# The last sum of a Mamba block, made by TensorE and copied out by ScalarE instead of added by GpSimd

## The chip, the cores and the metric

The kernel runs on one core of a Trainium2 chip. A core has five engines that each work through their own list of instructions in order and meet at semaphores: TensorE (PE in the profile, with its weight loads shown apart as PEld), VectorE (DVE), ScalarE (ACT), GpSimd (POOL) and SyncE (SP), which issues most of the DMAs. The metric is the device time of one execution in microseconds (us); lower is better. Of a kernel, the median of several executions counts.

## The reference

The reference is a stack of four layers on an input of 2 x 256 x 56 x 56 values: a windowed convolutional attention, a position term, a layer with a six-deep Mamba mixer and a selected-token feed-forward net, and a layer with a causal attention and a mixture of experts. The change touches one addition, the first `t + ...` of layer 2, where `_L2_attn_ref` ends in a root-mean-square norm:

```python
def _L2_attn_ref(x, norm_w, ..., norm_f_w):
    hidden, residual = x, None
    for i in range(n_layer):                      # 6
        residual = hidden if residual is None else hidden + residual
        hidden = rmsnorm(residual, norm_w[i])
        hidden = mamba_mixer(hidden, ...)          # projections, conv, selective scan, gate
    residual = hidden + residual
    return rmsnorm(residual, norm_f_w)
...
t = _to_tokens(x)
t = t + _L2_attn_ref(_ln_t(t), ...)                # <- this sum
t = t + _L2_ffn_ref(_ln_t(t), ...)
```

## The kernel before

The program has three phases: a convolution phase, a Mamba phase (about 700 to 7935 us of the profiled execution), and a tail with the two feed-forward nets and the last attention. All of it is float32.

**The Mamba phase.** A batch's 3136 tokens are cut into 7 chunks of 448 tokens; with 6 layers and 2 batches that makes 84 chunks, numbered by j in the order batch, layer, chunk. Channels lie on the 128 partitions. A chunk has 32 scan steps. A step is: `inputs` (a ScalarE copy of the old state, line 912, and a GpSimd product, line 913), `decays` (two ScalarE exponentials into a PSUM buffer `da`, line 896; three such buffers), `scan` (VectorE, line 934), `product` with C (line 926, on VectorE for 18 steps and on GpSimd for the 14 steps of `on_pool`), `keep` (a ScalarE copy of the last state, line 922), and `gather` (TensorE sums over the states into the PSUM buffer `acc`, line 949; `gate` on VectorE, line 963, takes it out).

**The projections of the next chunk run beside it.** They are pairs of a TensorE product into a PSUM buffer and a ScalarE instruction that takes it out: `u_project`/`u_keep`, `u_convolve`/`u_add`, `z_project`/`z_keep`, `x_project`/`x_keep`, `dt_project`/`dt_keep` (line 737, then two ScalarE instructions, lines 742 and 745), and `dt_add`/`dt_sum`. The last of these adds two tiles by two products with the identity matrix `ident` in one accumulation (lines 754 and 755) and copies the sum out by ScalarE (line 758). All of these pairs use one buffer: `mm()` takes it from the pool `mb_pmm`, which has one buffer, so each product waits until the previous pair's ScalarE instruction is done. Between `dt_keep` and `dt_add` stands `dt_softplus`, an exponential and a logarithm over all four blocks (lines 749 and 750, both ScalarE).

**The order is written out by hand.** Tables (`places`, `steps`, `last`) give each operation a place in units of scan steps within chunk j; all events are sorted by place and issued in that order, so each engine's list follows from the numbers. `dt_keep` of block 0 is at 18.43871, `dt_project` of block 2 at 19.28194, the `decays` of step 20 at 19.736.

**The last norm.** Two chunks after a chunk of the sixth layer, `spare` adds six more operations to chunk j by the table `last`: `l_squares` (5.88), `s_root` (6.46), `s_spread` (9.88), `l_weighted` (10.69), `f_load` (13.48), which loads the block's own input into the tile `t1`, and `l_out` (18.27). `l_weighted` (VectorE, line 803) makes the normed attention output `A["o"]`, 128 x 2 x 448; `l_out` adds it to `t1`, stores the sum to DRAM, and for the first batch starts the load of the next batch's residual into `res`. There are 14 such tails of chunks: 7 in the chunks j = 37 to 43 (first batch), 5 in j = 79 to 83 (second batch), and two in `rest`, a generator that the tail phase runs beside its own start, where `t1` lies in halves of the tile `hz`. The last of the 12, in j = 83, has no projections of a next chunk beside it. `o` shares one buffer with the tile `sq` of the squares.

```python
def l_out(j):
    nc.gpsimd.tensor_tensor(A["t1"], A["t1"], A["o"], ALU.add)          # 845
    nc.sync.dma_start(t2_v[A["b"], :, :, chunk(A["c"], T)], A["t1"])    # 846
    if A["b"] + 1 < B:
        nc.sync.dma_start(res[:, :, chunk(A["c"], T)], r_d[A["b"] + 1][A["c"]])   # 848
```

## Time and profile before

| | |
|---|---|
| median of 3 runs | 8862.84 us (8859.09 to 8866.49) |
| the profiled execution's own time | 8865.82 us |
| its span, first to last instruction | 8863.6 us |
| mean granted TensorE clock | 0.968 |
| DVE busy in the span | 7862.1 us (89%) |
| POOL busy in the span | 7621.6 us (86%) |
| PE busy in the span | 7448.6 us (84%) |
| ACT busy in the span | 6631.1 us (75%) |
| the 14 additions of line 845 | 2.07 to 2.11 us each |

The page of a profile gives busy times over the whole span, and the three phases differ. Between 700 and 7935 us, the Mamba phase, DVE was busy for 7059 of 7235 us, POOL for 7032, ACT for 6164 and PE for 6087. A busy share near one says that an engine is a candidate for the bound; what an engine's idle time waits for says whose lateness it pays for. In lines of the timeline, the columns are the start in us, the duration in us, the engine, the source line, the operation, output and inputs, shapes, and how many instructions are merged; a bracket gives the idle time before the first of them and who ended it. One matmul of the program in float32 appears as two records. A letter q behind an engine's name marks its sequencer (SPq: a DMA issued).

### The profile page before, as it was taken

The numbers are of one execution on the slowest core, as the hardware profiler recorded it, in microseconds if no ns is written. First come the engines' busy times: TensorE is split into PE (matmuls) and PEld (weight loads), VectorE is DVE, ScalarE is ACT, GpSimd is POOL, SyncE is SP. The second block draws the span as 40 slices with busy tenths as digits, with TensorE's granted clock in tenths as the row PEclk, the third lists the DMA queues.
The fourth block names the chain that finished last, engine by engine and source line by source line (L and its number), as shares of the span: only waits on it lengthen the run. The fifth ranks groups of instructions, "written<-read, shape, count | busy, mean of one in ns | idle before, by whom it ended". The sixth has DMA issues, their size and how long they took to land.

```text
span 8863.6 us, 106477 instructions
## 1 busy us (share of the span) xinstructions
PE 7448.6 (84%) x32350; PEld 3271.9 (37%) x32350; DVE 7862.1 (89%) x7216; ACT 6631.1 (75%) x15748; POOL 7621.6 (86%) x5327
## 2 busy tenths in 40 slices
PE   9988888888888888888888888888888888867986
PEld 6553333333333333333333333333333333325774
DVE  3339999999999999999999999999999999985763
ACT  1128888888888888888888888888888888863432
POOL 2329999999999999999999999999999999972336
PEclk9999999999999999999999999999999999978988
DMA  2235565565655565656566556556556565543224
GB/s 85 84 115 128 132 137 129 132 137 130 137 131 129 136 133 129 135 135 146 136 136 136 132 128 138 132 130 135 132 132 134 127 138 130 133 119 93 71 81 131
DMA packets 700485, 1118.30 MB, mean 126 GB/s; under 512 B 80508, under 2 KB 678083, under 8 KB 699907
## 3 DMA queue, kind: packets, MB, share of 16 engines
q1 hardware_dynamic: 685128, 1074.33, 52.4%
q0 software_dynamic: 14784, 37.18, 1.6%
q8 instruction: 257, 4.21, 0.2%
q14 instruction: 316, 2.59, 0.1%
HBM read 892.62 MB, written 218.60 MB: 125 GB/s over the span
## 4 chain that ended last, share of the span: by engine, by line
PE 44%; ACT 34%; DVE 12%; issue 7%; POOL 1%; DMA 1%; SPq 0%; ACTq 0%; POOLq 0%; DVEq 0%
ACT da L896 12%; PE mm L683 9%; PE mm L665 8%; PE mm L821 6%; DVE da L934 4%; PE acc L949 4%; DVE x L934 4%; ACT dt L742 2%; DVE x L926 2%; ACT hz L695 2%; ACT dt L750 2%; PE mm L754 2%; ACT hz L700 2%; ACT dt L749 2%; ACT dt L758 1%
## 5 line engine op out<-in xcount | busy, mean ns | idle before, releaser
L913 POOL TENSOR_TENSOR x<-dtur,bc 128x900 f32<-128x900 f32 x2688 | 4711.2, 1786 | 6.9 <-DMA dtu_d<-dtu 6.6
L896 ACT ACTIVATE da<-dtr,am 128x451 f32<-128x451 f32 x5376 | 3417.3, 641 | 322.4 <-DVE x L934 151.3
L934 DVE TENSOR_TENSOR_SCAN da<-da,x 128x902 f32<-128x902 f32 x1512 | 3040.3, 2031 | 97.4 <-ACT da L896 74.9
L934 DVE TENSOR_TENSOR_SCAN x<-da,x 128x902 f32<-128x902 f32 x1176 | 2343.5, 2020 | 45.8 <-ACT da L896 37.5
L926 POOL TENSOR_TENSOR x<-x,bc 128x896 f32<-128x896 f32 x1176 | 2074.3, 1777 | 80.7 <-DVE x L934 80.7
L926 DVE TENSOR_TENSOR x<-da,bc 128x896 f32<-128x896 f32 x1512 | 1606.2, 1076 | 19.1 <-ACT state L922 7.7
L949 PE MATMUL acc<-x,sum_w 128*32 128x448 f32 x10752 | 1380.2, 567 | 47.6 <-DVE x L926 30.2
L683 PE MATMUL mm<-u,w_cv 128*128 128x448 f32 x2656 | 1091.9, 553 | 67.1 <-ACT tail L678 56.9
L665 PE MATMUL mm<-xn,w_z 128*128 128x448 f32 x1332 | 588.8, 564 | 197.5 <-ACT dt L758 117.3
L683 PEld LDWEIGHTS mm<-u,w_cv 128*128 128x128 f32 x2656 | 478.4, 190 | 677.8 <-issue 373.8
L665 PE MATMUL mm<-xn,w_u 128*128 128x448 f32 x1328 | 580.8, 560 | 123.3 <-ACT hz L695 114.7
L821 PE MATMUL mm<-hz,w_out 128*128 128x448 f32 x1344 | 553.0, 554 | 107.9 <-ACT tail L678 56.3
L949 PEld LDWEIGHTS acc<-x,sum_w 128*32 128x32 f32 x10752 | 265.4, 111 | 954.9 <-issue 730.2
L754 PE MATMUL mm<-dt,mb_ident 128*128 128x448 f32 x666 | 342.6, 596 | 262.9 <-ACT state L922 148.6
L737 PE MATMUL mm<-xd,w_dt 128*128 128x448 f32 x664 | 341.1, 596 | 216.8 <-ACT dtu L745 128.5
L766 POOL TENSOR_TENSOR dtu<-dt,hz 128x448 f32<-128x448 f32 x336 | 329.4, 980 | 129.7 <-PE mm L755 81.9
L912 ACT COPY x<-state 128x2 f32<-128x2 f32 x2688 | 437.0, 187 | 0.0
L665 PEld LDWEIGHTS mm<-xn,w_z 128*128 128x128 f32 x1332 | 226.1, 189 | 566.4 <-ACT dt L758 237.8
L665 PEld LDWEIGHTS mm<-xn,w_u 128*128 128x128 f32 x1328 | 232.1, 189 | 460.4 <-ACT hz L695 226.7
L821 PEld LDWEIGHTS mm<-hz,w_out 128*128 128x128 f32 x1344 | 243.0, 191 | 417.5 <-issue 189.1
L695 ACT ACTIVATE hz<-mm,vec 128x448 f32<-128x448 f32 x332 | 209.0, 629 | 238.5 <-PE mm L683 234.0
L944 PE MATMUL acc<-hz,w_sk 128*128 128x448 f32 x672 | 347.4, 601 | 30.5 <-DVE hz L963 30.5
(366 smaller groups left out, 9520.3 us busy)
## 6 DMA issues: line engine op xcount, KB each, us to landing
dtr<-dt_d SPq DMA_DIRECT2D x1344, 224.0 KB, 4.4
dtur<-dtu_d SPq DMA_DIRECT2D x1344, 224.0 KB, 6.7
bc<-bc_d SPq DMA_DIRECT2D x336, 448.0 KB, 7.9
dt_d<-dt SPq DMA_DIRECT2D x336, 224.0 KB, 6.2
dtu_d<-dtu SPq DMA_DIRECT2D x336, 224.0 KB, 2.0
z_d<-out SPq DMA_DIRECT2D x56, 256.0 KB, 2.1
xg<-in_x SPq DMA_DIRECT2D x26, 448.0 KB, 9.2
bm<-in_edge SPq DMA_DIRECT2D x16, 539.0 KB, 4.4
```

The lines of the kernel that those rows point to most:

```text
L665: nc.tensor.matmul(ps, lhsT=w[:, k, chunk(d, P)], rhs=Q["xn"][:, k, :], start=(k == 0), stop=(k == 1),)
L683: nc.tensor.matmul(ps, lhsT=w_cv[:, 4 * d + k, :], rhs=M["u", d][:, k : k + T], start=(k == 0), stop=(k == 3),)
L695: nc.scalar.activation(hz(j)[:, d, :], M["mm"], AF.Identity, bias=layer_of(j + 1)["cb"][:, d : d + 1])
L754: nc.tensor.matmul(ps, lhsT=ident, rhs=M["dt"][:, d, :], start=True, stop=False)
L821: nc.tensor.matmul(ps, lhsT=layer_of(j - 1)["w_out"][:, d, chunk(k, P)], rhs=gated(j - 1)[:, d, :], start=(d == 0), stop=False,)
L896: nc.scalar.activation(D[i][:, chunk(g, R)], dtr[:, 2 * pr + g, :], AF.Exp, scale=L["am"][:, col : col + 1],)
L912: nc.scalar.copy(x[:, :, 0:1], states(i))
L913: nc.gpsimd.tensor_tensor(x[:, :, 1:], Q[k][1][:, 2 * pr : 2 * pr + 2, :], wide(Q["bc"][:, ng, :]), ALU.mult)
L926: engine.tensor_tensor(both(X[i])[:, :, 1 : T + 1], both(h)[:, :, 1 : T + 1], wide(QS[j]["bc"][:, 4 + ng, :T]), ALU.mult,)
L934: nc.vector.tensor_tensor_scan(h, D[i], X[i], 0.0, ALU.mult, ALU.add)
L944: nc.tensor.matmul(acc[0][:, :T], lhsT=L["w_sk"][:, k, :], rhs=Q["hz"][:, k, :], start=True, stop=False,)
L949: nc.tensor.matmul(acc[0][chunk(g, HD), :T], lhsT=sum_w, rhs=both(X[i - 1 + g // 2])[:, g % 2, 1 : T + 1], start=False, stop=(ng == 3), ti ...
```

## The change

The addition of `l_out` is made, for each half k of the tile, by two TensorE products with the identity into the buffer of `mm()`, and a ScalarE copy takes the sum back into `t1`. The place of `l_out` in the table `last` moves from 18.26579 to 18.60000, which is behind `dt_keep` of block 0 instead of between its `dt_project` and it. The two DMAs are as before; they now wait for the copy.

```diff
     def l_out(j):
-        nc.gpsimd.tensor_tensor(A["t1"], A["t1"], A["o"], ALU.add)
+        for k in range(2):
+            ps = M["mm"] = mm()[:, :T]
+            nc.tensor.matmul(ps, lhsT=ident, rhs=A["t1"][:, k, :], start=True, stop=False)
+            nc.tensor.matmul(ps, lhsT=ident, rhs=A["o"][:, k, :], start=False, stop=True)
+            nc.scalar.copy(A["t1"][:, k, :], ps)
         nc.sync.dma_start(t2_v[A["b"], :, :, chunk(A["c"], T)], A["t1"])
...
-        f_load: 13.47985, l_out: 18.26579,
+        f_load: 13.47985, l_out: 18.60000,
```

In the instruction lists, the changed kernel's ScalarE has the two copies, one straight behind the other, after line 745 of block 0 and one state copy of line 912, and ahead of a state copy of line 922 and the `decays` of step 20. TensorE has the four products between a `gather` and `dt_project` of block 2.

## The prediction

> **What bounds the kernel now.** I read the page's busy times first, then the waits of VectorE in the stretch of the Mamba phase that holds both groups of affected chunks (3810 to 7800 us), then the view of line 845 itself, and last the timeline of one affected place, engine by engine.

> ```profile
> PE 7448.6 (84%) x32350; PEld 3271.9 (37%) x32350; DVE 7862.1 (89%) x7216; ACT 6631.1 (75%) x15748; POOL 7621.6 (86%) x5327
> ...
> DVE da L934 <- ACT da L896: 38.9, 95, 0.8
> DVE x L934 <- ACT da L896: 22.7, 57, 1.8
> DVE o L803 <- PE mm L795: 17.4, 11, 1.6
> ...
> DVE da L934 <- POOL x L913: 2.0, 7, 0.3
> ```

> VectorE and GpSimd look equally full, but they are not equally the bound. In 3990 us VectorE waited 61.6 us for ScalarE's exponentials (line 896) and 2.0 us for GpSimd. So VectorE sets the pace, and what makes it late is ScalarE and the TensorE products that ScalarE waits for.

> ```profile
> L845 POOL TENSOR_TENSOR t<-t,o x12: 2086/2093/2109, 3901.2 to 7893.5; 128x896 f32<-128x896 f32 x12
> ...
> who waited for it (us, times):
>   ACT sq L776: 3.4, 1
> ```

> Of the twelve additions inside chunks, one made another engine wait. GpSimd has room behind the others: after the one at 3901.24 it idles 0.35 us for TensorE at 3917.59 and 2.60 us for VectorE at 3978.34. The chunk distance agrees. The starts of the SiLU of line 700 lie 85.31 us apart in ordinary chunks and 89.22 in affected ones. Of those 3.9 us, VectorE's timeline has 1.59 as the wait of line 803 for line 795 and 1.27 as line 803's own work at 3969.59, and most of the rest as two waits for ScalarE (0.42 at 3978.68, 0.34 at 3898.81); none is a wait for line 845.

> Now ScalarE where the copies go (j = 37):

> ```profile
> 3903.97 0.62 ACT L745 ACTIVATE u<-mm,above 128x448 f32<-128x448 f32 x1
> 3904.48 0.19 ACT L912 COPY x<-state 128x2 f32<-128x2 f32 x1
> 3904.56 0.17 ACT L922 COPY state<-da 128x2 f32<-128x2 f32 x1
> 3904.76 1.31 ACT L896 ACTIVATE da<-dtr,am 128x451 f32<-128x451 f32 x2
> ...
> 3909.61 1.79 ACT L749 ACTIVATE dt<-dt,cap 128x1792 f32<-128x1792 f32 x1
> 3911.43 1.79 ACT L750 ACTIVATE dt<-dt,one_col 128x1792 f32<-128x1792 f32 x1
> 3913.13 0.14 ACT L922 COPY state<-da 128x2 f32<-128x2 f32 x1
> 3913.31 1.32 ACT L896 ACTIVATE da<-dtr,am 128x451 f32<-128x451 f32 x2
> ...
> 3915.09 0.53 ACT L758 COPY dt<-mm 128x448 f32<-128x448 f32 x1 [0.20 <-PE mm L755]
> ```

> No bracket stands between 3904 and 3915: ScalarE has no idle time in these 11 us. And VectorE at the end of that run is already waiting for it:

> ```profile
> 3912.33 2.09 DVE L926 TENSOR_TENSOR x<-da,bc 128x896 f32<-128x896 f32 x2
> 3914.72 2.04 DVE L934 TENSOR_TENSOR_SCAN da<-da,x 128x902 f32<-128x902 f32 x1 [0.31 <-ACT da L896]
> ```

> **The change, part by part.** *Removed:* 14 additions on GpSimd, 12 x 2.09 + 2 x 2.07 = 29 us of its time. On the path I count them at nothing, because VectorE waited 2.0 us in all for GpSimd over both groups. Bounds: a gain of 12 x 2.09 = 25.1 us if GpSimd paced the chunks, nothing if VectorE does; I take nothing, by the waits.

> [...]

> *Added:* four matmuls and two copies per call. The nearest row is the same form of pair, `dt_add`/`dt_sum`:

> ```profile
> 3913.28 1.02 PE L754 MATMUL mm<-dt,mb_ident 128*128 128x448 f32 x2 [0.51 <-ACT state L922]
> 3914.14 0.91 PE L755 MATMUL mm<-u,mb_ident 128*128 128x448 f32 x2
> 3915.67 1.02 PE L754 MATMUL mm<-dt,mb_ident 128*128 128x448 f32 x2 [0.62 <-ACT state L922]
> ```

> From one pair to the next is 2.39 us: 1.81 from the first product's start to the copy (3913.28 to 3915.09), then 0.58 from the copy's start to the next product (to 3915.67), because `mm` has a single buffer. The busy time added is small (two copies of 0.53 on ScalarE), but both copies stand next to each other in ScalarE's list, so ScalarE stands still through both products. Step by step: `dt_project` of block 2 started at 3904.64 when line 745 gave the buffer back; the new product starts there instead. Copy one at 3904.64 + 1.81 = 3906.45, second product at 3907.03, copy two at 3908.84, and the next ScalarE instruction 0.43 us later (as 3915.09 to 3915.52) at 3909.27. It ran at 3904.56 before, so all that is queued behind is 4.71 us late. TensorE's `dt_project` of block 2 is late by 2 x 2.39 = 4.78, just inside ScalarE's own lateness.

> *Who waits behind it:* three pairs of `decays`, the `dt_keep` of two blocks, the softplus. VectorE has work in hand at first: the scan at 3908.33 uses the pair of 3904.76; a pair is ready 1.41 us after its start (3913.31 to 3914.72), so that scan starts at 3904.76 + 4.71 + 1.41 = 3910.88, 2.55 late. The next (pair at 3907.33) starts at 3913.45 instead of 3910.30, 3.15 late. The one at 3914.72 already waited, so it takes the whole 4.71. After it the brackets of ScalarE wait for TensorE's pairs, which are late by the same amount, and VectorE is again the full engine, with less than 3 us of waits in the rest of the chunk; I see nothing that gives time back. Bounds of one call: 0 (all regained) to 4.78; I take 4.71.

> *Moved:* the place 18.27 to 18.60 puts the call behind `dt_keep`, so `mm` stays in order. SP's two DMAs (3903.35 and 3903.83) now wait until about 3909.4; the next DMA in SP's list is `dt_d` at 3915.65, itself 4.7 us later then, so nothing queues up. The reloaded `res` is read three chunks later. `o` comes free when TensorE has read it, which only j = 83 notices.

> *The sum.* Eleven calls (j = 37 to 43 and 79 to 82) have the pattern above: 11 x 4.71 = 51.8 us. In j = 83 ScalarE waited 3.41 us for line 845 and VectorE 2.53 us for ScalarE; the copies take the place of that wait. Two pairs at full clock (4.8 us from about 7889.9) or half clock (some 8) put it between 1.2 us earlier and 2 later; I take 0. In `rest` the first call sits ahead of the tail's transposes on TensorE. They were paced by landings until 7945.25, so 4.8 to 8 us of products from 7935 are mostly covered: 0 to 4, I take 1.5. The second stands ahead of 14 ScalarE rows (line 1423, about 0.51 us each, 7961.41 to 7973.0) that used to run during the wait for `o` at 7966.3. ScalarE gets to them at about 7970.4 to 7973; 28 rows then end at 7984.7 to 7987.3 instead of 7981.7, and the chain of waits runs through the loads issued just behind (7982.13): 3 to 5.5, less if VectorE is what counts, so 0 to 5.5; I take 3.5. Total 51.8 + 0 + 1.5 + 3.5 = 56.8 us. On the profiled 8865.82 that gives 8922.6; on the median of 8862.84, 3 us lower, **8919.6 us** (+0.64%).

> Of the tail's clock: the granted clock was 0.50 from 7937 to 7949. [...]

> **Rivals.**
> - *GpSimd is the bound after all* (faster). Place: line 845 between products of line 913. For it: 98% busy in these stretches (586 of 600 us). Against it: 2.0 us of waits. It decides if the stall's 4.71 us is covered and VectorE follows GpSimd: 8862.8 - 25.1 = 8838, with the tail's 5 8843.
> - *The stall is hidden.* VectorE's work in hand and ScalarE's later idle times (0.20, 0.37, 0.49, 0.56, 0.43 = 2.05 us by 3927.6) would take up all of it. Against: those idle times wait for late products. Only the tail's 5 us remain: 8868.
> - *Half is regained.* If those 2.05 us count, 2.66 stay per call: 11 x 2.66 + 5 = 34, so 8897.
> - *It costs more.* If later gathers or `decays` of the next chunk (line 867's loads behind `dt`) slip too, 6 us per call and 5.5 + 4 + 2 at the end: 77, so 8940.

> **How the numbers follow.** Forecast 0.68; half regained 0.13; more 0.08; hidden 0.06; GpSimd 0.05. Below 0.2% (17.7 us) a measurement of this kernel tells nothing. The forecast, half and more are slower (0.89); hidden is the same (0.06); GpSimd faster (0.05). The forecast's own range is 8908 to 8928: 11 x 4.3 to 11 x 4.78 with the tail between -1.2 and 11.5. The stated range goes down to the half case and a little up: 8893 to 8932.

> **What would show it.** Line 845's successors at two copies per call, the second starting 2.4 us behind the first; ScalarE's idle before them about 1.9 us each; affected chunks 93.9 us apart instead of 89.2; a wait of VectorE of some 2.5 us at the scan of step 20 and further ones, about 4.7 in sum, all for line 896; GpSimd's idle time up by some 6.8 us per affected chunk. Chunks still 89.2 apart would prove the forecast wrong, and chunks near 87 the first rival right.

## The result, and the profile after

The changed kernel took 8942.99 us, median of 6 runs (8928.0 to 8946.24), against 8863.61 us of the kernel before (6 runs on the same chip, 8859.09 to 8867.58). The ratio is 1.0086, 95% interval 1.0076 to 1.0097: 0.86% slower, where 0.64% was forecast, and 11 us above the range. The profiled execution took 8944.72 us with a span of 8942.6, 79 us more than before's.

Lines move down by four behind the diff: line 896 is now 900, 913 is 917, 926 is 930, 934 is 938. The page of the changed kernel first (engine, busy us, share of the span; then groups with busy us and mean ns, idle time and its releaser):

```profile
PE 7511.5 (84%) x32462; PEld 3298.4 (37%) x32462; DVE 7862.5 (88%) x7216; ACT 6648.0 (74%) x15776; POOL 7596.4 (85%) x5313
...
L917 POOL TENSOR_TENSOR x<-dtur,bc 128x900 f32<-128x900 f32 x2688 | 4717.2, 1792 | 45.8 <-PE acc L953 38.4
...
L766 POOL TENSOR_TENSOR dtu<-dt,hz 128x448 f32<-128x448 f32 x336 | 330.8, 985 | 163.2 <-PE mm L755 114.5
```

VectorE's work is unchanged (7862.5 against 7862.1 us busy), and all of the loss is waiting. GpSimd is 25 us less busy, but it now idles for TensorE: 163 us ahead of `dtu`, where it was 130. The waits of VectorE in the same stretch as in the prediction, 3810 to 7800 us (total, times, longest):

```profile
DVE da L938 <- ACT da L900: 83.2, 114, 2.5
DVE x L938 <- ACT da L900: 27.9, 62, 1.8
DVE o L803 <- PE mm L795: 15.8, 10, 1.6
...
DVE da L938 <- POOL x L917: 3.7, 5, 2.3
```

The first two rows, VectorE waiting for ScalarE's exponentials, grew from 61.6 to 111.1 us, and the longest of the first from 0.8 to 2.5. The wait is where the prediction put it. The view of the new copies (minimum, median and maximum in ns; then what they waited for, and who for them):

```profile
L849 ACT COPY t<-mm x24: 520/532/533, 3910.9 to 7963.1; 128x448 f32<-128x448 f32 x24
...
its engine sat idle before it (us, times) until:
  PE mm L848: 56.4, 27
who waited for it (us, times):
...
  PEld mm L737: 14.8, 11
```

28 copies wait 56.4 us for their products, 2.0 each. One call in full, that of j = 38, as ScalarE ran it (start, duration, line; a bracket is idle time and its releaser):

```profile
4004.56 0.62 ACT L745 ACTIVATE u<-mm,above 128x448 f32<-128x448 f32 x1
4005.08 0.19 ACT L916 COPY x<-state 128x2 f32<-128x2 f32 x1
4007.04 0.53 ACT L849 COPY t<-mm 128x448 f32<-128x448 f32 x1 [1.78 <-PE mm L848]
4009.43 0.53 ACT L849 COPY t<-mm 128x448 f32<-128x448 f32 x1 [1.86 <-PE mm L848]
4009.86 0.17 ACT L926 COPY state<-da 128x2 f32<-128x2 f32 x1
4010.06 1.31 ACT L900 ACTIVATE da<-dtr,am 128x451 f32<-128x451 f32 x2
```

The copies stand 2.39 us apart, with 1.78 and 1.86 us of idle time, as forecast. VectorE behind them:

```profile
4011.48 2.04 DVE L938 TENSOR_TENSOR_SCAN da<-da,x 128x902 f32<-128x902 f32 x1 [2.47 <-ACT da L900]
4013.97 2.04 DVE L938 TENSOR_TENSOR_SCAN da<-da,x 128x902 f32<-128x902 f32 x1 [0.45 <-ACT da L900]
...
4020.02 2.04 DVE L938 TENSOR_TENSOR_SCAN da<-da,x 128x902 f32<-128x902 f32 x1 [1.88 <-ACT da L900]
4023.89 2.04 DVE L938 TENSOR_TENSOR_SCAN x<-da,x 128x902 f32<-128x902 f32 x1 [1.82 <-ACT da L900]
```

Against the same chunk of before, the first of these scans is 2.55 us late, the second 3.10, the third 4.70. The prediction had 2.55, 3.15 and 4.71, and then nothing more. But there is a fourth wait: 1.82 us, where before had 0.23, and the lateness is 6.29. TensorE shows why (two records are one product):

```profile
4012.51 1.02 PE L737 MATMUL mm<-xd,w_dt 128*128 128x448 f32 x2 [1.47 <-ACT dtu L745]
...
4018.58 1.86 PE L754 MATMUL mm<-dt,mb_ident 128*128 128x448 f32 x2 [2.66 <-ACT state L926]
4020.24 1.70 PE L755 MATMUL mm<-u,mb_ident 128*128 128x448 f32 x2
4022.56 1.02 PE L754 MATMUL mm<-dt,mb_ident 128*128 128x448 f32 x2 [0.62 <-ACT dt L758]
4023.42 0.91 PE L755 MATMUL mm<-dtu,mb_ident 128*128 128x448 f32 x2
```

The first `dt_add` pair took 1.86 and 1.70 us, the next one, the same instructions, 1.02 and 0.91. The view by windows gives the reason (columns: window, its length, busy us of PE, PEld, DVE, ACT and POOL, then the granted TensorE clock, the DMA share and GB/s):

```profile
4015.20:4018.60 3.40, 0.74 (x9) 0.02 (x1) 2.91 (x3) 3.34 (x3) 3.36 (x2) 1.00 0.00 0
4018.60:4022.00 3.40, 3.34 (x4) 1.16 (x4) 1.98 (x1) 1.57 (x6) 0.17 (x1) 0.50 0.00 0
4022.00:4025.40 3.40, 2.22 (x5) 0.97 (x6) 1.58 (x2) 3.00 (x10) 0.92 (x1) 1.00 0.18 67
```

The clock was halved for one window of 3.4 us, after one in which TensorE worked only 0.74 us because it waited for ScalarE, which was in the softplus, and the half-clock window fell on the pair that ScalarE and VectorE wait for: 1.59 us.

**Where the 79.1 us lie.** Starts of the SiLU of line 700 mark the chunks; one lies between two calls. Distances in us that hold the calls of j = 37 to 43, and 79 to 81 (before, then after):

| | 37 | 38 | 39 | 40 | 41 | 42 | 43 | 79 | 80 | 81 |
|---|---|---|---|---|---|---|---|---|---|---|
| before | 89.22 | 89.22 | 91.10 | 92.22 | 89.22 | 89.22 | 85.45 | 89.22 | 91.17 | 89.22 |
| after | 96.12 | 95.51 | 95.48 | 97.97 | 95.79 | 96.01 | 90.56 | 95.94 | 96.16 | 95.48 |

| stretch | forecast | after less before |
|---|---|---|
| from the start to the first call | 0 | +4.5 |
| the ten calls of the table | 47.1 | +59.8 |
| chunks between the two groups | 0 | -1.9 |
| calls of j = 82 and 83 and those in `rest`, up to the loads of `chan` in the tail | 9.7 | +8.7 |
| from there to the end | 0 | +8.0 |
| sum | 56.8 | +79.1 |

### The profile page after: what moved, and what is told of

Read it like the earlier page. It is cut to its first block, busy times and chain, and to the rows that moved or that the text cites. A ratio compares the mean times of both kernels' runs of the same rounds, so it can differ in the third digit from the quotient of the medians.

```text
span 8942.6 us, 106741 instructions
## 1 busy us (share of the span) xinstructions
PE 7511.5 (84%) x32462; PEld 3298.4 (37%) x32462; DVE 7862.5 (88%) x7216; ACT 6648.0 (74%) x15776; POOL 7596.4 (85%) x5313
## 4 chain that ended last, share of the span: by engine, by line
PE 45%; ACT 33%; DVE 13%; issue 6%; DMA 1%; POOL 1%; SPq 0%; ACTq 0%; POOLq 0%; DVEq 0%
ACT da L900 11%; PE mm L683 9%; PE mm L665 8%; PE mm L821 6%; DVE da L938 4%; PE acc L953 4%; DVE x L938 4%; ACT dt L742 2%; DVE x L930 2%; PE mm L754 2%; ACT hz L695 2%; ACT dt L750 2%; ACT hz L700 2%; ACT dt L749 2%; ACT dt L758 1%
## 5 line engine op out<-in xcount | busy, mean ns | idle before, releaser
L938 DVE TENSOR_TENSOR_SCAN x<-da,x 128x902 f32<-128x902 f32 x1176 | 2341.6, 2018 | 51.8 <-ACT da L900 42.7
L754 PE MATMUL mm<-dt,mb_ident 128*128 128x448 f32 x666 | 346.0, 602 | 267.6 <-ACT state L926 147.3
```

The source lines that it names most:

```text
L754: nc.tensor.matmul(ps, lhsT=ident, rhs=M["dt"][:, d, :], start=True, stop=False)
L938: nc.vector.tensor_tensor_scan(h, D[i], X[i], 0.0, ALU.mult, ALU.add)
```

## The experiments

The chips that ran these gave the kernel before 8907 to 8921 us, more than the first chip. The chunk distances of the unchanged parts agree with the first chip's to some 0.02 us; the additional time lies in the tail, behind the loads of `chan`, for every kernel. So each time is compared with the kernel before on its own chip, and chunk distances with the table above.

**Chunks and rest apart.** `l_out` as changed in the chunks alone, and in `rest` alone (`nj` is the number of chunks, 84):

```diff
     def l_out(j):
+        if j == nj:                                    # rest_only: if j < nj
+            nc.gpsimd.tensor_tensor(A["t1"], A["t1"], A["o"], ALU.add)
+        else:
...
```

> Twelve calls as changed, the two in rest added by GpSimd as before. Stall theory (ScalarE stands still behind two products that share one buffer, 4.7 us per call, and TensorE's half-clock windows add 0 to 2.2 us per call): affected chunks 95 to 96.5 us apart, total 8925 to 8934. Rival, the two calls in rest cost nothing and the end of the trace differs by chance: total 8938 to 8946, like the full change.

> The two calls in rest as changed, the twelve in chunks added by GpSimd as before. Theory: the last part, from the last gather to the end, is 5 to 13 us longer than before, total 8868 to 8876, and affected chunks are 89.2 us apart. Rival (the end differs by chance): total 8860 to 8867.

Measured: chunks alone 8985.41 against 8919.93 us, 1.0066 (1.0049 to 1.0083); rest alone 8934.42, 1.0012 (1.0002 to 1.0022). Most of the loss is the chunks'. The distances of the ten calls, chunks alone: 95.80, 96.03, 94.46, 96.91, 95.31, 94.47, 90.01; 96.10, 95.23, 96.16. Rest alone has the chunk distances of before, and reaches the loads of `chan` 6.6 us later than before, counted from the start of the last chunk.

With the chunks alone, two calls, j = 40 (96.91) and j = 43 (90.01), have no window with a halved clock in their chunk. The view by windows of the chunk of j = 40 (granted clock 1.00, the third figure from the end), then its first `dt_add` pair and two of VectorE's scans (here line 941):

```profile
4187.00:4283.90 96.90, 78.19 (x313) 31.17 (x313) 86.36 (x59) 80.61 (x200) 84.32 (x56) 1.00 0.60 141
```
```profile
4211.28 1.02 PE L754 MATMUL mm<-dt,mb_ident 128*128 128x448 f32 x2 [2.66 <-ACT state L929]
4212.14 0.91 PE L755 MATMUL mm<-u,mb_ident 128*128 128x448 f32 x2
```
```profile
4212.72 2.04 DVE L941 TENSOR_TENSOR_SCAN da<-da,x 128x902 f32<-128x902 f32 x1 [1.87 <-ACT da L903]
4215.41 2.04 DVE L941 TENSOR_TENSOR_SCAN x<-da,x 128x902 f32<-128x902 f32 x1 [0.65 <-ACT da L903]
```

The pair takes 1.02 and 0.91 us here. Against the same chunk of before, the scans are 2.55, 3.10 and 4.69 us late, and then stay 4.69 late to the chunk's end: 96.91 is 4.69 over 92.22. For j = 43, 90.01 is 4.56 over 85.45. So the whole sum at full clock costs what was forecast for one call.

**No sum at all.** The addition is left out, and `o` is stored (at the changed place, 18.60).

```diff
-        nc.gpsimd.tensor_tensor(A["t1"], A["t1"], A["o"], ALU.add)
-        nc.sync.dma_start(t2_v[A["b"], :, :, chunk(A["c"], T)], A["t1"])
+        nc.sync.dma_start(t2_v[A["b"], :, :, chunk(A["c"], T)], A["o"])
```

> The sum is left out on every engine: the normed attention output alone is stored as t (the tail then works on other values). Theory that the addition on GpSimd cost nothing inside chunks: affected chunks 89.2 us apart, total 8858 to 8864 (a little off in j = 83 and in rest). Rival (GpSimd paces the chunks): 87.1 us apart, total about 8838.

Measured: 8919.36 us, ratio 0.9997 (0.9987 to 1.0006). VectorE's waits from 3810 to 7800 us:

```profile
DVE da L933 <- ACT da L895: 40.4, 100, 0.9
DVE x L933 <- ACT da L895: 21.6, 58, 1.8
DVE o L803 <- PE mm L795: 17.4, 11, 1.6
```

These are 40.4 and 21.6 us, where before had 38.9 and 22.7 with the additions. Chunks of 89.22 us before take 89.22 to 89.30 here, where no second half-clock window falls in them. GpSimd's 2.09 us per call were free, and the rival "GpSimd is the bound" is refuted: nothing was there to be gained.

**The copies taken apart and moved.** The sum written as two separate pairs half a chunk later (places 32.51 to 34.66), each copy with other ScalarE work between it and its product; `l_weighted` writes into `res`, so that the tile lives long enough.

```diff
+                for k, (at_sum, at_keep) in enumerate(((32.513, 33.45), (34.23, 34.65))):
+                    put(j * ns + at_sum, l_sum, j, k)
+                    put(j * ns + at_keep, l_keep, j, k)
+                put(j * ns + 34.66, l_store, j)
```

> The same products and copies for eleven calls, but moved about one half chunk later and taken apart: first product at 32.51, its copy at 33.45, second product at 34.23, its copy at 34.65, in gaps of the buffer and with other ScalarE work between product and copy; the normed output is written over its place in res, so that it can wait. The call in j = 83 and the two in rest are as in the change. Stall theory: affected chunks 89.2 to 90.5 us apart, total 8868 to 8890. Rival (the added work on TensorE and ScalarE is the price, wherever it stands): 94 to 96 us apart, total 8930 to 8945.

Measured: 8983.51 us, 1.0068 (1.0051 to 1.0085), no better than the chunks alone (1.0066). The stall theory's 89.2 to 90.5 us failed. Distances of the ten calls: 96.23, 94.52, 96.22, 99.20, 94.52, 96.21, 90.62; 96.22, 96.16, 94.57. ScalarE in the call of j = 38 (here the copies are line 860):

```profile
4041.02 0.53 ACT L860 COPY t<-mm 128x448 f32<-128x448 f32 x1 [0.53 <-PE mm L857]
...
4043.41 0.53 ACT L677 COPY u<-mm 128x448 f32<-128x448 f32 x1 [1.43 <-PE mm L665]
...
4046.39 0.52 ACT L860 COPY t<-mm 128x448 f32<-128x448 f32 x1
...
4051.03 0.53 ACT L828 COPY res<-mm 128x448 f32<-128x448 f32 x1 [4.03 <-PE mm L825]
```

The copies themselves wait 0.53 us and not at all. But the pairs behind them are late: `y_keep` (line 828) waits 4.03 us for a product that used to keep it 0.27 us. That product itself waited 1.14 us for the second copy to give the buffer back. VectorE pays it in one piece (TensorE's product of line 821 first, then VectorE):

```profile
4046.97 3.27 PE L821 MATMUL mm<-hz,w_out 128*128 128x448 f32 x8 [1.14 <-ACT t L860]
```
```profile
4054.10 2.04 DVE L951 TENSOR_TENSOR_SCAN da<-da,x 128x902 f32<-128x902 f32 x1 [4.55 <-ACT da L913]
```

Where no half-clock window stands (j = 41, 94.52), the call costs 5.3 us, more than the 4.7 at its first place. So ScalarE's standing still at that place isn't the price. A theory that fits is that of the chain: all pairs go through the one buffer `mm`, so TensorE and ScalarE take turns on a single chain, and what is added to it makes all later pairs late, wherever it stands.

**The chain tested by its length.** Three kernels, made from the changed one. First the place moved to 21.45, where the first product runs beside the softplus:

```diff
-        f_load: 13.47985, l_out: 18.60000,
+        f_load: 13.47985, l_out: 21.45000,
```

> One number changed against the change: l_out at 21.45 instead of 18.60 (18.60 kept for j = 83), so that the first product runs while ScalarE is in the softplus and only the second pair lies open. Theory (a call costs what it adds to the chain of pairs through the one buffer of mm): the first product is covered, 0.6 + 2.4 = 3.0 us remain, affected chunks 92.2 us apart where TensorE's clock stays full and up to 94 where it does not. Rival (the lateness of ScalarE's copies is the same anywhere): 93.9 to 96.

Measured: 8948.52 against 8907.35 us, 1.0043 (1.0026 to 1.0060). Five of the ten distances are 92.23 or 92.24, 3.01 us over 89.22; the one of 94.16 (j = 41) has a half-clock window at 68.6 us that these lack. ScalarE in the call of j = 38:

```profile
4004.71 1.79 ACT L750 ACTIVATE dt<-dt,one_col 128x1792 f32<-128x1792 f32 x1
4006.40 0.51 ACT L849 COPY t<-mm 128x448 f32<-128x448 f32 x1
4008.78 0.53 ACT L849 COPY t<-mm 128x448 f32<-128x448 f32 x1 [1.86 <-PE mm L848]
```

The first copy finds its product ready (no bracket): that pair adds only the 0.53 us of the copy and part of a handover, the second its full 2.4.

Second, half of the sum by TensorE, the other half added by GpSimd:

```diff
-        for k in range(2):
+        for k in range(1):
...
+        nc.gpsimd.tensor_tensor(A["t1"][:, 1, :], A["t1"][:, 1, :], A["o"][:, 1, :], ALU.add)
```

> Half of the tile (k = 0) is summed by TensorE and ScalarE as in the change, the other half by GpSimd. Theory: one pair in the chain costs 2.4 us at full clock, affected chunks 91.6 us apart, plus up to 1.6 where a half-clock window falls on a pair. Rival (the call has a fixed cost, from the moved place or the first wait, and the second pair adds little): 93 to 96.

Measured: 8954.03 us, 1.0051 (1.0033 to 1.0070); distances 91.53, 93.11, 91.54, 95.57, 93.00, 91.54, 87.62; 93.10, 91.52, 94.65. The four at 91.5 are 2.31 over before: one pair, one price. Those at 93.1 have a half-clock window from 21.4 to 21.8 us behind the SiLU, and cost 1.5 to 1.6 more.

Third, the four products kept, the copies taken out, and the sum made by GpSimd as before:

```diff
-            nc.scalar.copy(A["t1"][:, k, :], ps)
+        nc.gpsimd.tensor_tensor(A["t1"], A["t1"], A["o"], ALU.add)
```

> The four products into the buffer of mm stay, the two copies are left out, and GpSimd makes the sum as before the change. Theory (TensorE's time in the chain): dt_project of block 2 starts 3.5 us late, without the two handovers, and affected chunks are 92.8 us apart plus the clock's part. Rival (ScalarE's standing copies are the price): 89.2 to 89.8.

Measured: 8970.80 us, 1.0065 (1.0048 to 1.0081); distances 92.59, 97.54, 92.57, 95.58, 92.58, 92.58, 93.64; 92.58, 92.57, 97.54. The usual 92.58 is near the theory's 92.8 and far from the rival's 89.2 to 89.8. The products alone lengthen the chain by 3.36 us; the rest up to 4.70, 1.34 us, goes with the two handovers to the copies. Since there is no copy to wait for here, the 3.36 us are TensorE's own time ahead of `dt_project`. Whether a buffer of its own for the sum would save the 1.34 us wasn't tested. And two chunks with the same instructions as their neighbours take 4.96 us more, 97.54. The first of them, the window ahead of the half clock and the half clock itself (columns as above):

```profile
4009.90:4013.30 3.40, 1.17 (x3) 0.67 (x4) 1.80 (x2) 3.30 (x5) 3.40 (x3) 1.00 0.01 3
4013.30:4026.90 13.60, 11.73 (x18) 3.72 (x20) 9.24 (x5) 7.83 (x23) 9.15 (x7) 0.50 0.55 130
```

TensorE was busy 1.17 of 3.4 us, and then had half the clock for four windows in a row, 13.6 us, over two of the four `dt_add` pairs and the products between them; the neighbour at 92.57 has no half clock at all.

**The half clock attacked.** In the changed kernel, two short products are put ahead of the first `dt_add` pair, so that TensorE isn't idle before it:

```diff
         ps = M["mm"] = mm()[:, :T]
+        if d == 0 and j > 1 and chunks[j - 2][1] == NL - 1:
+            for _ in range(2):
+                fill(ps)
```

> The change, with two idle products into the fresh mm buffer in front of dt_add of block 0 in the affected chunks, where TensorE otherwise idles 2.7 us behind the softplus. Theory (the surplus over 4.7 us per call is TensorE at half clock for 3.4 us after a window in which it was busy less than half): the half-clock windows 18 to 25 us behind the SiLU of line 700 vanish, affected chunks come to 93.9 to 94.6 us apart (95.5 where the second window, 69 us behind, still comes). Rival (the surplus is a late gather or load, not the clock): 95.5 to 96.1 as before.

Measured: 8980.13 us, 1.0072 (1.0055 to 1.0089), no measurable difference from the chunks alone; distances 96.03, 96.15, 95.62, 98.61, 96.11, 95.57, 90.00; 96.03, 96.14, 95.58. The expectation failed. The half-clock window at 24.3 us is gone, but others stand at 18.0 to 18.7 and 68.7 to 72.2 us, and they cost the same. The one call without a half-clock window in its chunk, j = 43 (90.00), costs 4.55 us, as in the chunks alone. No kernel with the whole sum kept all ten chunks free of half clock.

**The opposite edit, in every chunk.** If two pairs cost 4.7 us, does taking one out of the chain give 2.4 back? In the kernel before, the sum of one of the `dt` blocks (0, 1 or 2) is made by GpSimd. A chunk has four such pairs, one for each block, and not three as the expectations say:

```diff
     def dt_add(j, d):
+        if d in (0,):                                  # (1,) and (2,) in the other two
+            nc.gpsimd.tensor_tensor(M["dt"][:, d, :], M["dt"][:, d, :], over[d], ALU.add)
+            return
...
     def dt_sum(j, d):
-        nc.scalar.copy(M["dt"][:, d, :], M["mm"])
+        if d not in (0,):
+            nc.scalar.copy(M["dt"][:, d, :], M["mm"])
```

> The kernel before with the opposite edit in every chunk: of the three pairs through mm that add the two halves of dt (dt_add and dt_sum), the first (block 0) is taken away from TensorE and ScalarE, and GpSimd makes that sum as one 128x448 addition of about 1 us ahead of its dtu product. Theory of the chain (a pair costs its 2.4 us only as far as VectorE waits for what is behind it): VectorE waits about 0.3 + 0.2 + 0.45 us per ordinary chunk for ScalarE, so 0.2 to 0.5 us of 85.31 are to be had: chunks of 84.8 to 85.1, ratio 0.995 to 0.998; the half-clock window then no longer stays at one place of the chunk (85.31 is 25.0 windows) and single chunks may be longer. Rival, GpSimd is full: VectorE waits for it, chunks of about 86.3, ratio 1.009. Rival, nothing: chunks of 85.3.

> As the kernel with block 0 of dt on GpSimd, but for block 1: the pair in the middle is taken from the chain and its sum made by GpSimd. Theory of the chain: the same 0.2 to 0.5 us per chunk, since length and not place counts (ratio 0.995 to 0.998). Rival, GpSimd is full: ratio about 1.009. If the place counts, this kernel and the one of block 0 differ by more than 0.3 us per chunk.

> As the two kernels before it, but for block 2, the last pair of the three: what stands behind it in the chain is brought forward by 2.4 us, what stands ahead of it is not. Theory of the chain: VectorE's first waits of a chunk (0.3 + 0.2 us, for the exponentials next to the pairs) stay and only the later ones can shrink, so 0 to 0.3 us per chunk (ratio 0.997 to 1.000). Rival, GpSimd is full: ratio about 1.009.

Measured against 8920.91 us (9 runs): block 0 8967.2, 1.0052 (1.0038 to 1.0066); block 1 8979.07, 1.0060 (1.0046 to 1.0074); block 2 8958.59, 1.0044 (1.0031 to 1.0058). All are slower; the gain that I expected of the chain isn't there. The shortest distances are 85.46, 85.31 and 85.48 us against 85.30 of before. With block 0, GpSimd shows up in VectorE's waits from 1000 to 3700 us:

```profile
DVE da L938 <- ACT da L900: 25.0, 62, 0.8
DVE x L938 <- POOL x L917: 13.2, 32, 0.5
DVE x L938 <- ACT da L900: 6.2, 10, 1.4
```

The last row was 13.6 us before, and 13.2 us for GpSimd stand in its place: 0.4 us per chunk, where the rival of a full GpSimd had 1.0. With block 1, GpSimd isn't what VectorE waits for (1.4 us in the same stretch), and an ordinary chunk is exactly as long as before. Its loss is another, the clock and what hangs on it:

```profile
1000.00:3700.00 2700.00, 2265.53 (x8578) 857.12 (x8571) 2614.53 (x1741) 2288.24 (x5485) 2636.15 (x1611) 0.96 0.59 131
```
```profile
DVE xn L807 <- PE mm L799: 18.6, 7, 4.2
```

The second row was 0.9 us before. The mean granted clock fell from 0.99 to 0.96, and the chunks where a layer gives way to the next, where line 803 (here 807) waits for line 795 (799), take 90.8 to 92.8 us instead of 88.3 to 88.5. Between the SiLUs of the second chunk and the last, TensorE spent 147 us at half clock in the kernel before, and 485, 590 and 413 us in these three.

## Why the prediction was wrong, and where it was right

*Right: what bounds the kernel, and the removed additions at nothing.* Without any sum the ratio is 0.9997; both ends were named (0 and 25.1 us), and the one taken held. One reading of the rival's evidence was off: "586 of 600 us" is GpSimd in stretches of ordinary chunks; from 3800 to 4400, with the first affected group, it was busy for 573.6.

*Right: the stall and whom it meets.* Copies 2.39 us apart, idle times of 1.78 and 1.86, scans late by 2.55, 3.10 and 4.70 (forecast 2.55, 3.15, 4.71), each wait for line 896 (now 900). GpSimd's idle time in the chunk of j = 38 rose by 8.2 us, from 3.5 to 11.7; 6.8 was forecast, and the rest goes with the 1.6 us of the half-clock pair. The three lower rivals (GpSimd the bound, hidden, half regained) are out.

*Wrong: the term "11 x 4.71 = 51.8".* The first ten of these eleven calls are those of the first table; they cost 59.8 us, 5.98 each, against 47.1. The step that failed is the price of one call, and in it the sentence "From one pair to the next is 2.39 us": it took every product at the duration of the one place that it was read from (1.02 and 0.91 us, at a granted clock of 1.00), and so put the half clock at nothing. The runs show in its place a price of 4.7 for the chain, as forecast, plus the half-clock windows that now fall on pairs which VectorE waits for. Of the 59.8 us, 46.9 are the chain (4.70 for eight calls, 4.69 and 4.56 for j = 40 and 43, from the chunks without half clock above) and 12.9 the half clock, 16.7 after less 3.8 before:

- j = 38, 39 and 81: one window, at 24.3 us, on the first `dt_add` pair, +1.58. 89.22 + 4.70 + 1.58 = 95.50; measured 95.51, 95.48 and 95.48.
- j = 37, 41, 42, 79 and 80: one at 18.0 to 18.6 us, on `dt_project`, +0.5, and one at 69.2 to 69.8 us, on `u_convolve`, +1.6. The sum is 96.0; measured 95.79 to 96.16. In j = 37, VectorE's scans are 5.26 us late behind the first window and 6.90 behind the second.
- j = 40: one at 24.4 us, +1.06 (97.97). j = 43: one at 18.0 us, +0.55 (90.56).
- Before had a second window only in j = 39 and 80 (91.10 and 91.17), +1.9 each.

The second pattern in the call of j = 37, first TensorE and then the windows:

```profile
3913.90 1.02 PE L737 MATMUL mm<-xd,w_dt 128*128 128x448 f32 x2 [0.62 <-ACT t L849]
3916.38 1.86 PE L737 MATMUL mm<-xd,w_dt 128*128 128x448 f32 x2 [1.47 <-ACT dtu L745]
```
```profile
3912.80:3916.20 3.40, 1.49 (x4) 0.30 (x2) 0.93 (x2) 2.82 (x6) 3.40 (x3) 1.00 1.08 196
3916.20:3919.60 3.40, 3.22 (x4) 1.17 (x4) 2.95 (x2) 2.87 (x8) 0.43 (x1) 0.50 0.71 258
```

The product at 3916.38 takes 1.86 us and the one 2.5 us ahead of it 1.02; between them the granted clock goes from 1.00 to 0.50. That these windows are the surplus is shown by chunks of one kernel that differ in nothing else (92.57 and 97.54 with the products alone, 91.53 and 93.1 with one half), by records of about twice the length (1.86 against 1.02 us), and by the two calls of the chunks alone that have no such window and cost 4.69 and 4.56.

The prediction counted the half clock only at the end (some 8 us instead of 4.8 for the two pairs of j = 83 and of `rest`, and 0.50 from 7937 to 7949), not in the ten calls; "I see nothing that gives time back" was right, and what was missing was to look for what takes more.

*The rival "It costs more"* had the size (6 us per call, 8940) but another mechanism, later gathers and loads of the next chunk. The gathers did come later: from 3810 to 7800 us GpSimd waited 35.5 us for them, where before has no such row. But VectorE waited only 3.7 us for GpSimd there (2.0 before), so this isn't where the 12.7 us beyond the forecast lie. The rival's near hit on the total is luck.

*The calls of j = 82, 83 and `rest`.* 9.7 us forecast, 8.7 measured up to the loads of `chan`. The bounds held. With the products in `rest` the half clock there was shorter: before had it for 13.7 us from 7936, rest alone has none there, and the changed kernel 3.4 us; the two calls cost 6.6 us all the same (rest alone).

*Not explained by the change.* 4.5 us lie before the first call, where both kernels run the same instructions; in the other eight runs with the same instructions there, this stretch differs from before's by -1.6 to +7.0. 8.0 us lie behind the loads of `chan`; the same stretch of four experiments on one chip differs by 11 us (against before's on the first chip it was 64.5 us longer for the chunks alone, 64.1 for rest alone, 64.6 without the sum, 53.6 for the moved copies), so it can't be laid to the sum. Of the 22.3 us that the forecast lacked in the profiled executions, 12.7 are the ten calls, and 12.5 are these two stretches; the others take 2.9 back. Without either of the two, the time would have been about 8930, inside the range that went up to 8932, so only a part of the miss is the half clock's. (The upper end of the forecast's own range sums to 8927, not 8928; nothing hangs on it.) Whether the last 8.0 have to do with the two calls of `rest` stays open: rest alone costs 0.12% (0.02 to 0.22), some 11 us, of which 6.6 were found ahead of `chan`.

## What to carry to other kernels

Pairs of a product and a copy through a single PSUM buffer acted here as one chain over two engines: what was added to it cost its whole length (two handovers included) where the bound engine hung on that chain, 4.7 us at one place of the chunk and 5.3 at another, and only work that fitted under something longer on the chain, as the softplus here, was cheaper. It doesn't follow that taking a pair out wins: here an addition of a pair cost 2.3 us, and removal of one brought nothing, where VectorE was busy for 2645 of 2700 us already. And with the change of TensorE's load the half-clock windows moved (from 15 us behind line 700 to 18.0 to 18.6 and 24.3 to 24.4 in the changed chunks), so price such a change also with the products that the bound engine waits for at half clock (1.86 us against 1.02 here).
